# A fused AdaLN block of attention and FFN in fp32: the row maxima go from score rows to subtraction through DRAM, all loads go to SyncE's queue, the prologue joins the written order, and that order is new

## The chip, the cores and the metric

The kernel runs on one core of a Trainium2 chip. The core has five engines with queues of their own: TensorE (PE, matrix products and transposes by a product with the identity), VectorE (DVE), ScalarE (ACT), GpSimd (POOL) and SyncE (SP), which in this kernel does nothing but start DMAs. ACT can start DMAs too. PE reads its operands from SBUF and writes to PSUM, which has eight banks of 2 KB per partition.

The metric is the time of one execution in device microseconds (us), the median of several.

## The reference, cut to what matters

```python
mod = (_silu(L0_c) @ L0_wmod).reshape(8, 6, 1, 256)
sa, ca, ga, sb, cb, gb = (mod[:, k] for k in range(6))
ga = (2 * (ga >= 0) - 1) * jnp.maximum(jnp.abs(ga), 0.25)   # gb likewise
h = _layernorm(x) * (1 + ca) + sa                      # x: (8, 1024, 256)
scores = jnp.einsum('nsd,ntd->nst', h * w_lhs, h * w_rhs)
x = x + ga * jnp.einsum('nst,ntd->nsd', softmax(scores, axis=2), h)
h = _layernorm(x) * (1 + cb) + sb
x = x + gb * (relu(h @ W1 + b1) @ W2 + b2)             # 256 -> 1024 -> 256
```

Everything is fp32. There are eight batches of 1024 rows. The score matrix of a batch is symmetric, since both sides carry the same `h` and the two weights only multiply its columns.

## The kernel before, in words

**Tiles.** The 1024 rows of a batch are `NT` = 8 tiles of `P` = 128 rows; two halves of `HALF` = 512 rows (`g` = 0, 1) are loaded, stored and given to the FFN as one. `V` = 32 is the side of the blocks that DVE's transpose turns.

**Attention of one batch.** Of the scores, PE computes the upper part of the matrix (L520), ACT copies it out of PSUM (L529), and the lower part is its mirror: DVE transposes the 32 × 32 blocks into `T_m` (L555), SP writes them to DRAM as `D_m` in four DMAs (L393) and reads them back in their new places into `sc` (L399). Batch 0 mirrors by PE (L577) instead. For the product with `h` the index that is summed over must lie in the partitions; by the symmetry, the subtraction therefore works on the columns of the matrix that answer to a row tile, 8 blocks with the other index in the partitions and the 128 rows along the free dimension. So the maximum `m` of a row tile, 128 values in 128 partitions (`row_max`, DVE, L603), has to stand along the free dimension of every partition: `max_turn` (L606) lets PE transpose the broadcast column into a bank, `pm` (L608), and `subtract` (L611, DVE, L615) subtracts it from these 128 × 1024 scores with `pm` read from PSUM. ACT takes the exponential (L624).

Two rows form a pair for the product with `h`: `pair_begin` (`pp`, L692; sums into `W`, L701 and L704), `left_sums` (POOL, L717 and L722, the sums `s` of the two exponentials), `pair_end` (`pr` and `pq`, L746: the products are saved Strassen-fashion by sums of operands), `pair_out` (DVE, L763 to L786: divides by the row sum and adds to `x`).

**FFN.** Its input is normed, transposed through DRAM in 32 × 32 blocks (DVE `T_f`, L405; four writes `D_f`, L393; one read `X_f`, L399), modulated into `hT` (L898 on DVE, L900 on ACT) and into POOL's sums `hs` (L911). The first layer is made of the units `pa`, `pb`, `pe` (L923), whose sums DVE adds up (L944), ACT passes through the relu (L1005) and POOL sums further into `ft` (L1019). The second layer is `ya`, `yb`, `yc` (L923); DVE adds them to `Y` (L1049) and so frees the banks, and POOL adds the result to `x` (L1122); `y_out` (L1125) stores 512 KB. The last batch does its second layer otherwise: it loads gated weights `w2g` and `rows` (`load_last`, L1131) and multiplies directly (`py`, L1161).

**Preparation of the next batch.** While batch b is in its attention, the rows of batch b+1 are loaded (`load_x`, L168; six half-batch buffers), normed (DVE statistics L324, ACT L330 to L363), transposed through DRAM like the FFN's input (`T_a`, `D_a`, `X_a`), and multiplied by gate rows (POOL L849, L853) that `load_rows` (L318) spreads over the partitions, 256 KB, into one of two buffers. `load_x` and `load_rows` are issued on ACT's queue by default.

**Order.** Four tables of tokens, `ZERO`, `FIRST`, `MIDDLE` (five times) and `LAST`, give the order of everything after the prologue. `period` (L1457) goes through a table; each token takes the next part of one piece of work, and `:n` names the PSUM bank. A period holds the attention of batch b, most of the FFN of batch b−1 and the preparation of batch b+1. `pin` (L147) then makes every engine execute its instructions in just this order, so an instruction that waits holds all that stand behind it on its engine. The tokens needed below: `S`, `H` score products; `M` mirror parts; `R` row maximum; `T` the spreading of the maximum; `U` subtraction; `E` exponential; `B`, `C`, `L`, `D`, `O` the pair's steps; `a`, `b`, `e` first-layer units; `y*` second layer, with `yo` the store; `fk` and `fh` the FFN's transposition and `hT`; `lx`, `lr` the loads of `x` and of gate rows; `xp` POOL's first use of these; `lw` the load for the last layer. A `+` marks work of the next batch.

The prologue (L1197 to L1305: loads, modulation, norms and transposes of batch 0, first scores) is straight-line code ahead of the tables, in which `any_bank` hands out PSUM banks in turn and three warming matmuls of zeros (L227) stand around the transposes of `c` (L243).

Of the kernel before, what the change touches and what calls it, by code (L numbers as in the profile page):

```python
# [19 lines left out]
GATE_MIN = 0.25  # L20
ZERO = """
pa1 pa1 pa0 pa1 R2 H3:3 N2:4 M2:0 E1 H5:7 lx0 N2 M2 H4:1 S3:6 H5 p0:7 pa0 pa1 pa0 S3 H4
pr1 H3 M5:4 pa0 T2:5 g:1 M4:0 M3:2 pr0 R3 pn0 pn1 U2 M3 pn0 pn0 pn0 p0 M5 pn1 pn0 E2 g
pn1 T3:3 R4 p1:2 U3 pb0 p0 p1 pn1 T4:5 p2:3 M4 H6:6 pb0 pb0 E3 pn1 U4 E4 H6 pb1 pb1 pb0
p1 pb1 R6 R5 p2 M6:7 p3:4 p3 p1 p2 pb1 T6:3 T5:1 pl0 U5 pl0 p2 H7:2 m:6 px0 M6 U6 H7 px0
E5 R7 p4:0 S1+:2 p4 m p3 p4 pl1 pl1 T7:7 px1 E6 U7 p0 p3 S0+:3 px1 H0+:1 H1+:5 S0+ p5:6
fr0 H1+ S1+ E7 H0+ M1+ M0+ R0+ fn0 p5 p7:5 p6:3 p5 fn0 fn0 fn0 fh0 p4 xp1 xp1 xt0 xt0 ps
xt1 fh0 fh0 p7 p6 p6 p7 fh0 xp0 M1+ M0+ p5 p7 p6 xp0 xp0 xp0 xt0 xt0 xt1 xt1 xt1 fh0 rs
rs rs xp1 M0+ M1+ rs xp1 fh0
"""  # L30
FIRST = """
a00:1 S3:4 H2:3 T0:0 lx1 S2:6 S3 b00:5 fr1 pa0 fn1 H2 fn1 pa0 R1 fn1 H3:3 a00 S2 e02:4
b00 T1:2 a00 fn1 H3 a02:3 a00 R2 pa0 U0 pa0 M3 M2 M2 e00:6 a00 H4:5 fn1 e00 lr e00 U1
a00 E0 a00 H4 pr0 a02 r00 pn0 fk1 e02 fk1 pn0 E1 b02:5 e00 b02 a02 B0:0 e02 pa1 C0 M3 L0
pa1 a00 pn0 pn0 a02 e02 M4 M2 M3 fk1 fk1 M4 H5:5 a02 D0:1 D0:2 a02 R3 l02 pn0 pb0 pb0
r02 pb0 B0 C0 l00 L0 D0 L0 D0 t02 T2:6 H5 ya0:7 L0 t00 t02 a02 a02 t00 U2 E2 ya0 yb0:5
O0 T3:6 D0 R4 t00 O0 ya0 B2:0 ya0 fh1 U3 E3 a10:6 ya0 O0 pa1 M5 t02 yb0 pa1 O0 fh1 fh1
t00 L2 fh1 xp0 D2:5 ya0 ya0 t02 xt0 pr1 pn1 O0 a10 pn1 pn1 M4 M5 pb0 yc0:4 pn1 ya0 pn1
H6:2 C2 B2 yc0 pb1 pb1 L2 T4:1 D2:7 yc0 C2 xp0 fh1 fh1 xt0 L2 xt1 L2 a10 D2 R5 yg0 H6
a10 T5:0 U4 D2 D2 yc0 M6 e10:3 pb1 e12:2 M5 O2 Q0 O2 M6 U5 b10:1 b10 O2 E4 pl0 px0 yg0  # L40
e10 pl0 a10 a10 H7:0 B4:4 yt0 E5 r10 e12 px0 O2 O2 Q0 pb1 M6 yt0 yt0 a12:1 C4 a12 e10
e10 a12 e12 a12 b12:7 l10 B4 H7 yt0 xp0 b12 Q2 Q2 R6 xt0 L4 a12 D4:3 D4:7 xt1 xt0 t10 ps
L4 L4 L4 t10 pl1 yd0 px1 C4 a12 e12 a10 D4 S0+:4 D4 T6:2 fr0 a10 fn0 R7 O4 t10 yd0 t10
U6 r12 l12 t12 a12 D4 O4 T7:2 ya1:5 O4 U7 pl1 px1 E6 H0+:6 fn0 a12 S0+ ya1 E7 S1+:4
yb1:7 t12 H0+ fn0 fn0 xt1 xp0 B6:6 C6 ya1 L6 t12 xt1 xp1 H1+:1 O4 M0+ fn0 t12 S1+ O4 Q4
fk0 yb1 fk0 B6 ya1 yc1:3 ya1 ya1 M0+ fk0 D6:7 R0+ T0+:0 ya1 fk0 fh0 yc1 Q4 M0+ yo0 yg1
H1+ U0+ D6:4 yc1 C6 yc1 lx0 E0+ yg1 ya1 fh0 L6 L6 xp1 D6 D6 O6 fh0 L6 D6 R1+ M1+ O6 O6
fh0 rs rs fh0 M1+ fh0 xp1 xp1 rs rs O6 M1+ yt1 O6 yt1 Q6 Q6 yt1 yt1
"""
MIDDLE = """  # L50
S2:2 H3:6 a00:3 b00:5 H2:0 a00 S2 B0:2 H2 e00:1 T1:0 C0 B0 e00 S3:4 a00 a00 fr1 M2 b00
C0 pa0 pa0 a02:2 U1 a02 lr pa0 fn1 H4:5 e00 pa0 a00 e00 a00 e02:7 a02 R2 E1 pr0 fn1 H4
a00 L0 b02:5 S3 H3 fn1 fn1 fn1 D0:1 a00 M3 L0 yd1 b02 M2 fk1 e02 a02 r00 a02 e02 D0:6
l00 pn0 a02 e02 l02 M2 pn0 yd1 L0 t00 T2:0 D0 t00 t00 a02 D0 L0 U2 R3 fk1 O0 M4 yo1 M3
ya0:3 D0 T3:5 M3 H5:4 fk1 U3 lx1 pn0 a02 r02 t02 ps t02 ya0 O0 pn0 ya0 H5 pn0 yb0:5 ya0
E3 O0 pa1 pb0 fk1 pb0 pb0 M4 M4 pa1 ya0 t02 t02 H6:7 O0 pa1 R4 fh1 M5 O0 yb0 E2 Q0 ya0
xp0 t00 xt0 fh1 fh1 fh1 fh1 fh1 L2 H6 ya0 B2:4 ya0 yc0:0 M6 T4:3 C2 yc0 U4 pa1 pb0 pl0
pr1 M6 D2:5 a10:1 a10 M5 M5 b10:2 D2:6 yc0 pn1 R5 pn1 pn1 B2 yg0 pn1 pn1 E4 px0 pl0 L2
L2 D2 L2 pb1 D2 a10 a10 D2 pb1 b10 C2 yc0 O2 a12:3 O2 O2 O2 B4:0 e10:4 T5:6 a10 pb1 a12
e10 px0 M6 O2 pb1 R6 U5 a10 a12 e10 C4 E5 a10 e10 a12 yg0 Q2 a10 e12:4 a12 Q2 xp0 L4 L4  # L60
xp1 H7:1 L4 L4 xt0 xt1 e12 pl1 a12 e12 D4:2 e12 b12:6 D4:5 T6:7 a12 S0+:4 b12 D4 B4 Q0
yt0 H7 px1 r12 r10 a12 l12 l10 px1 U6 E6 fr0 xt0 R7 D4 yt0 D4 C4 yt0 yt0 pl1 O4 fn0 O4
O4 fn0 fn0 H0+:3 T7:7 S1+:0 fn0 O4 U7 S1+ S0+ fn0 H0+ E7 yb1:6 B6:7 xp0 t12 xt1 t10 xp0
t10 H1+:5 t12 t10 xt0 L6 yd0 yd0 t10 L6 ya1:3 D6:4 C6 ya1 ya1 D6:1 xp1 t12 rs t12 L6 L6
fk0 M0+ fk0 yb1 O4 B6 D6 R0+ C6 ya1 M0+ fk0 yo0 M0+ fk0 ya1 T0+:7 yc1:6 ya1 ya1 D6 yc1
fh0 U0+ H1+ O6 M1+ M1+ fh0 R1+ yc1 yc1 fh0 xt1 xp1 xp1 xt1 rs rs fh0 fh0 fh0 rs D6 yg1
ya1 lx0 yg1 E0+ O6 yt1 O6 Q4 Q4 yt1 O6 O6 Q6 M1+ yt1 Q6 yt1
"""
LAST = """
b00:2 S3:6 H2:0 S2:3 H2 a02:5 T1:0 e00:1 B0:7 a00:4 S2 e00 fr1 C0 e00 M2 R2 U1 S3 a00  # L70
a00 b00 a00 e00 a02 B0 E1 H3:3 a00 fn1 C0 a00 fn1 H3 b02:0 b02 M3 l00 e02:1 H5:6 a00 a02
L0 e02 fn1 H5 fn1 a02 e02 T2:7 a02 H4:3 M2 M2 M3 yd1 M3 fn1 a02 a02 D0:2 a00 fk1 fk1 L0
L0 yd1 yo1 r02 r00 t00 H4 a02 e02 M5 U2 yb0:3 D0:6 D0 fk1 M4 fk1 M4 M5 R3 R4 l02 E2 t00
B2:1 H6:7 T3:5 t00 t02 fh1 L0 t02 H6 ya0:0 D0 O0 fh1 D0 O0 O0 M6 O0 ya0 U3 M4 M6 yb0 O0
C2 ya0 b10:6 ya0 t02 B2 fh1 fh1 E3 t02 ya0 ya0 t00 yc0:7 T4:4 Q0 M5 L2 fh1 L2 yc0 U4 ya0
e10:2 L2 R6 a10:4 L2 fh1 a10 yc0 D2:5 a10 b10 C2 yc0 E4 yg0 R5 ya0 e10 a10 yg0 yt0 yt0
D2:0 D2 e10 e10 D2 a12:7 O2 Q0 D2 O2 O2 a12 l10 O2 a10 a12 a10 r10 e12:0 H7:6 T5:2 e12
H7 O2 U5 a10 a10 Q2 B4:1 Q2 a12 e12 a12 t10 yt0 yt0 E5 C4 b12:5 M6 fr0 B4 fn0 a12 a12
r12 R7 e12 b12 l12 fn0 a12 C4 t10 L4 L4 yd0 D4:2 L4 L4 D4:3 D4 D4 O4 T7:5 fn0 fn0 fn0 D4
T6:1 U6 E6 U7 fk0 O4 fk0 E7 t10 O4 t12 yd0 yb1:7 lw yo0 ya1:6 B6:5 t12 ya1 ya1 ya1 fk0  # L80
fk0 L6 t12 D6:4 L6 C6 D6:0 D6 ya1 O4 t10 L6 D6 O4 fh0 fh0 B6 ya1 yb1 C6 L6 t12 yc1:1 yc1
D6 O6 O6 O6 O6 Q4 yc1 Q4 O6 Q6 ya1 lw fh0 e00+:7 a00+:5 Q6 fh0 lw lw fb fh0 lw a02+:3
b00+:0 fr1+ a00+ b00+ a00+ ya1 e00+ lw a00+ fh0 e00+ fn1+ e00+ b02+:0 yc1 a00+ e02+:1
a02+ a00+ l00+ e02+ r00+ a02+ a00+ fn1+ a02+ fn1+ fn1+ yg1 lw fb e02+ lw e02+ b02+ fb lw
a02+ z3:2 a00+ z0:7 fn1+ fk1+ fk1+ z2:1 a02+ fk1+ fk1+ z1:4 a02+ r02+ l02+ z2 a02+ z0
fh1+ z3 fh1+ fh1+ e10+:0 a10+:6 e10+ yg1 a10+ yt1 z0 fh1+ fb fh1+ fh1+ z1 b10+:3 fb fb
fb b10+ z3 yt1 yt1 z2 a10+ e10+ a10+ z1 e10+ a12+:2 a10+ e12+:4 a12+ a12+ a10+ a10+
b12+:5 fb b12+ e12+ l10+ a12+ a12+ e12+ a12+ a10+ e12+ z5:5 r10+ z6:6 a12+ r12+ l12+
a12+ z4:7 z6 z4 z5 z4 z6 z5 z3 yt1 yd1+ yd1+ yo1+ z6 z1 z5 z7:3 z7 z7 z7
# [5 lines left out]
def adaln_block_kernel(  # L95
# [43 lines left out]
    turn = deque([4, 5, 6, 3, 7])  # L139

    def any_bank(name):
        turn.rotate(-1)
        return bank(turn[-1], name)

# [23 lines left out]
    def load_x(b, g, queue=nc.scalar):  # L168
        x_t[b, g] = ring(two, [P, TH, D], "x", 6, f"x_{b}_{g}", 2 * b + g)
        queue.dma_start(  # L170
            out=x_t[b, g],
            in_=x[b, ts(g, HALF), :].rearrange("(t p) d -> p t d", p=P),
        )
# [194 lines left out]
    def prepare_norm(b, g, tiles=range(TH)):  # L368
# [85 lines left out]
    def prepare_turn(b, g, vector=True):  # L454
# [26 lines left out]
        return left  # L481

# [1022 lines left out]
```

## Time and profile before

| | us |
|---|---|
| median of 3 runs (756.27 to 761.42) | 759.52 |
| profiled execution, whole | 760.63 |
| profiled execution, span from first to last instruction | 758.8 |
| POOL `s` 128x512 (L717), mean of 28 | 1.27 |
| PE second-layer or first-layer matmul 128x256 (L923), mean | 0.38 |
| DVE maximum of a row tile (L603), mean of 64 | 1.20 |
| ACT exponential of a row tile (L624), mean of 64 | 1.06 |

In the profile, a line such as `L603 DVE TENSOR_REDUCE m<-sc 128x1 f32<-128x1024 f32 x64 | 76.7, 1200 | 1.6 <-ACT sc L529 1.6` says: the instruction of line 603 on DVE read `sc` (128 partitions by 1024 elements) and wrote `m`; 64 of them were busy 76.7 us, 1200 ns each; the engine stood idle for 1.6 us just ahead of them, and what ended this was ACT's writing of `sc`. In a timeline, the columns are start (us), duration (us), engine, line, operation, out<-in and how many instructions run as one group; a group's duration reaches from the start of its first to the modelled end of its last, so neighbouring groups of PE overlap. A DMA line says how many were issued, the size of one, and the median time from issue to landing. The traffic with DRAM is 124 GB/s over the span, and one profiled issue on SP lasts 0.43 us in the median; before, SP issues 496 DMAs and ACT 20.

### The profile page before, as it was taken

Reading aid. Unit: us, or ns where it says so; the run is one execution under the profiler, and the core shown is the slowest. Engines: PE = TensorE matmul, PEld = TensorE weight load, DVE = VectorE, ACT = ScalarE, POOL = GpSimd, SP = SyncE. Lnnn points to the kernel's source line nnn. Section 1 sums busy time; section 2 is a strip of 40 time slices with the busy share of each in tenths; the row PEclk is TensorE's granted clock in tenths of the full one; section 3 lists DMA queues with packets and bytes.
Section 4 is the critical chain, followed back from the end, with each engine's and each line's share of the span. In section 5 each row is a group of like instructions: output and inputs, shape, how many; then the busy total and the mean of one; then the engine's idle time right before and its main releaser. Section 6 shows DMA issues by size and latency. Waiting matters only on the chain.

```text
span 758.8 us, 11945 instructions
## 1 busy us (share of the span) xinstructions
PE 748.0 (99%) x4044; PEld 626.8 (83%) x4044; DVE 527.7 (70%) x1138; ACT 394.5 (52%) x741; POOL 506.7 (67%) x509
## 2 busy tenths in 40 slices
PE   8999999999999999999999999999999999998998
PEld 4687789788888888887898888978888888987887
DVE  7886877858785786848877587767868586674431
ACT  4562746536465465635657254663656446361541
POOL 3723695957849685696838968399684967577231
PEclk9999999999999999999999999999999999999999
DMA  8134333256525554255632655335552645114122
GB/s 307 43 111 117 105 112 98 65 152 187 155 67 153 172 162 115 71 169 165 184 96 78 181 160 160 99 104 177 166 142 65 183 119 147 30 52 153 28 80 88
DMA packets 106213, 95.22 MB, mean 125 GB/s; under 512 B 29700, under 2 KB 98848, under 8 KB 106152
## 3 DMA queue, kind: packets, MB, share of 16 engines
q1 hardware_dynamic: 98408, 85.81, 39.7%
q10 hardware_dynamic: 7744, 8.65, 3.6%
q8 instruction: 32, 0.52, 0.3%
q14 instruction: 29, 0.24, 0.1%
HBM read 50.62 MB, written 43.81 MB: 124 GB/s over the span
## 4 chain that ended last, share of the span: by engine, by line
PE 89%; DVE 5%; DMA 3%; SPq 1%; ACT 1%; issue 1%; POOL 0%; DVEq 0%; ACTq 0%; POOLq 0%
PE psc L520 16%; PE pa L923 13%; PE ya L923 11%; PE pr L746 9%; PE pe L923 7%; PE pq L746 6%; PE yc L923 6%; PE pp L692 6%; PE po L641 4%; PE py L1161 4%; PE pb L923 3%; PE yb L923 3%; DVE f L944 1%; PE pm L608 1%; DVE pT L615 1%
## 5 line engine op out<-in xcount | busy, mean ns | idle before, releaser
L520 PE MATMUL psc<-rT,lT 128*128 128x512 f32 (+3 forms) x384 | 137.1, 486 | 0.0
L717 POOL TENSOR_TENSOR s<-pT 128x512 f32<-128x512 f32 x28 | 35.6, 1270 | 109.8 <-ACT pT L624 107.7
L520 PEld LDWEIGHTS psc<-rT,lT 128*128 128x128 f32 x384 | 67.0, 191 | 36.0 <-issue 24.4
L615 DVE TENSOR_TENSOR pT<-sc,pm 128x1024 f32<-128x1024 f32 x64 | 77.3, 1208 | 18.9 <-PE pm L608 9.4
L603 DVE TENSOR_REDUCE m<-sc 128x1 f32<-128x1024 f32 x64 | 76.7, 1200 | 1.6 <-ACT sc L529 1.6
L624 ACT ACTIVATE pT<-pT 128x1024 f32<-128x1024 f32 x64 | 67.1, 1056 | 14.8 <-DVE pT L615 12.0
L1005 ACT ACTIVATE f<-f 128x512 f32<-128x512 f32 (+1 forms) x64 | 52.2, 844 | 31.4 <-DVE f L944 31.4
L923 PE MATMUL pa<-hT,w 128*128 128x256 f32 x256 | 66.1, 381 | 0.8 <-DVE f L944 0.4
L911 POOL TENSOR_TENSOR hs<-hT 128x256 f32<-128x256 f32 x32 | 23.1, 731 | 63.3 <-DVE hT L898 58.0
L923 PE MATMUL pa<-hs,w1s 128*128 128x256 f32 x256 | 64.8, 379 | 0.0
L529 ACT COPY sc<-psc 128x512 f32<-128x512 f32 (+3 forms) x96 | 44.2, 479 | 38.1 <-PE psc L520 36.5
L692 PEld LDWEIGHTS pp<-xg,pT 128*128 128x128 f32 x448 | 56.9, 192 | 6.2 <-issue 2.4
L692 PE MATMUL pp<-xg,pT 128*128 128x129 f32 x448 | 59.1, 275 | 0.7 <-DVE Y L1049 0.7
L746 PEld LDWEIGHTS pq<-tsum,pT 128*128 128x128 f32 x448 | 57.4, 192 | 2.3 <-issue 0.2
L746 PE MATMUL pq<-tsum,pT 128*128 128x128 f32 (+1 forms) x448 | 59.1, 275 | 0.0
L939 ACT COPY k<-pa 128x512 f32<-128x512 f32 x64 | 36.8, 581 | 40.5 <-PE pa L923 33.9
L923 PE MATMUL yc<-f,w2s 128*128 128x256 f32 x224 | 54.1, 385 | 3.5 <-DVE Y L1049 3.5
L849 POOL TENSOR_TENSOR x<-x,rows 128x256 f32<-128x256 f32 x64 | 46.3, 734 | 11.7 <-ACT rows L1274 10.0
L1019 POOL TENSOR_TENSOR ft<-f 128x512 f32<-128x512 f32 x28 | 35.7, 1275 | 27.6 <-ACT f L1005 27.6
L923 PEld LDWEIGHTS pa<-hT,w 128*128 128x128 f32 x256 | 46.0, 190 | 9.6 <-issue 2.4
L923 PE MATMUL ya<-ft,w 128*128 128x256 f32 x224 | 53.6, 383 | 0.0
L923 PEld LDWEIGHTS pa<-hs,w1s 128*128 128x128 f32 x256 | 46.7, 190 | 6.6 <-ACT k L939 0.2
(161 smaller groups left out, 1761.3 us busy)
## 6 DMA issues: line engine op xcount, KB each, us to landing
D_f<-T_f SPq DMA_DIRECT2D x60, 128.0 KB, 2.4
X_f<-D_f SPq DMA_DIRECT2D x15, 512.0 KB, 3.4
D_a<-T_a SPq DMA_DIRECT2D x56, 128.0 KB, 2.4
D_y<-T_y SPq DMA_DIRECT2D x56, 128.0 KB, 2.6
Y<-D_y SPq DMA_DIRECT2D x14, 512.0 KB, 3.4
out_dram<-x SPq DMA_DIRECT2D x14, 512.0 KB, 4.3
X_a<-D_a SPq DMA_DIRECT2D x13, 512.0 KB, 3.7
x<-in_L_attn_x_dram ACTq DMA_DIRECT2D x12, 512.0 KB, 3.7
```

What stands on the lines that cost most here:

```text
L520: nc.tensor.matmul(psc[:, : hi - lo], lhsT=lT_t[b, i // TH][:, k, ts(i % TH, P)], rhs=rT_t[b, n][:, k, lo - n * HALF : HALF], start=(k == ...
L529: nc.scalar.copy(score_row(b, i)[:, lo // V : hi // V, :], box["p"][:, : hi - lo].rearrange("p (n v) -> p n v", v=V),)
L603: nc.vector.tensor_reduce(m, score_row(b, i), AX.XY, ALU.max)
L615: nc.vector.tensor_tensor(pT.rearrange("p j (a v) -> p j a v", v=V), score_columns(b, i), pm[:, :P].rearrange("p (j a v) -> p j a v", j=1, ...
L624: nc.scalar.activation(pT_t[b, i], pT_t[b, i], AF.Exp)
L692: nc.tensor.matmul(box["pp"][:, h * XS : (h + 1) * XS], lhsT=pT_t[b, i][:, h * TH + t, :], rhs=xg_t[b][:, h * TH + t, P : P + XS], start=( ...
L746: nc.tensor.matmul(out, lhsT=lhs[:, t, :], rhs=rhs[:, t, :], start=(t == 0), stop=(t == TH - 1),)
L849: nc.gpsimd.tensor_tensor(xr, xr, rows_t[b][:, 1, :], ALU.add)
L923: nc.tensor.matmul(out, lhsT=lhsT, rhs=rhs, start=first, stop=True, skip_group_check=True)
L939: nc.scalar.copy(k, src)
L1005: nc.scalar.activation(part, part, AF.Relu)
L1019: nc.gpsimd.tensor_tensor(out, x, y, op)
```

## The change

- **The maximum's way.** For batches 1 to 7 `max_turn` is gone. `row_max` writes the maxima of the two rows of a pair into the two columns of one 128 × 2 tile. `max_rows` writes this tile to DRAM (8 bytes from each partition) and reads the 256 values back into every partition, 128 KB, as `mr`; both DMAs are SP's. `subtract` reads its row out of `mr` (every second element) in SBUF. The token `T` exists for even rows only and has two parts, write and read. Batch 0 keeps the transposes.
- **The loads.** `load_x` and `load_rows` are issued by SP; the gate rows have one buffer instead of two.
- **The prologue** is cut into parts with tokens of their own and stands in the table `ZERO`; `any_bank` and the straight-line code go. In it, the transposes of `c` (`0c`) come ahead of the three warming matmuls (`0w`).
- **The tables** are all new. Middle table before: `lr` is token 26, `yo1` 86, `lx1` 95. After: `yo1` 54, `lx1` 82, `lr` 163. In the last table the store `yo0` moves from the place just ahead of `lw` and of the FFN's writes to the end of the table.

The arithmetic is unchanged, and so is the number of all other instructions of DVE and POOL.

```diff
-    def load_x(b, g, queue=nc.scalar):
+    def load_x(b, g, queue=nc.sync):
...
     def rows_tile(b):
-        rows_t[b] = ring(two, [P, 2, D], "rows", 2, f"rows_{b}", b)
+        rows_t[b] = ring(two, [P, 2, D], "rows", 1, f"rows_{b}", b)
         return rows_t[b]

-    def load_rows(b, queue=nc.scalar):
+    def load_rows(b, queue=nc.sync):
...
     def row_max(b, i):
-        m = ring(work, [P, 1], "m", 3, f"m_{b}_{i}")
+        if (b, i // 2) not in max_t:
+            max_t[b, i // 2] = [ring(work, [P, 2], "m", 3, f"m_{b}_{i}", (b * NT + i) // 2)]
+        m = max_t[b, i // 2][0][:, i % 2 : i % 2 + 1]
         nc.vector.tensor_reduce(m, score_row(b, i), AX.XY, ALU.max)
-        max_t[b, i] = m
-
-    def max_turn(b, i, q=2):
+
+    def max_turn(b, i, q):
+        m = max_t[b, i // 2][0][:, i % 2 : i % 2 + 1]
         pm = bank(q, f"pm_{b}_{i}")
-        nc.tensor.transpose(pm[:, :P], max_t.pop((b, i)).to_broadcast([P, P]), ident)
-        pT_t[b, i] = pm
+        nc.tensor.transpose(pm[:, :P], m.to_broadcast([P, P]), ident)
+        pT_t[b, i] = pm[:, :P]
+
+    def max_rows(b, i):
+
+        at, box = (b * NT + i) // 2, {}
+
+        def write():
+            box["D"] = ring(dram, [P, 2], "M", 4, f"M_{b}_{i}", at)
+            nc.sync.dma_start(out=box["D"], in_=max_t[b, i // 2][0])
+
+        def back():
+            R = ring(work, [P, P, 2], "mr", 2, f"mr_{b}_{i}", at)
+            nc.sync.dma_start(
+                out=R.rearrange("p s r -> p (s r)"),
+                in_=box["D"].rearrange("s r -> (s r)").partition_broadcast(P),
+            )
+            for r in range(2):
+                pT_t[b, i + r] = R[:, :, r]
+
+        return [write, back]
...
     def subtract(b, i):
...
             score_columns(b, i),
-            pm[:, :P].rearrange("p (j a v) -> p j a v", j=1, v=V).to_broadcast([P, NT, NV, V]),
+            pm.rearrange("p (j a v) -> p j a v", j=1, v=V).to_broadcast([P, NT, NV, V]),
             ALU.subtract,
...
         for i in range(0 if b == 1 else 1, NT):
-            w[f"T{i}"] = [lambda q, i=i: max_turn(b, i, q)]
+            if i % 2 == 0:
+                w[f"T{i}"] = max_rows(b, i)
             w[f"U{i}"] = [lambda i=i: subtract(b, i)]
...
-            w["T0+"] = [lambda q: max_turn(n, 0, q)]
+            w["T0+"] = max_rows(n, 0)
```

The stretch of the middle table from the first maximum of the second pair to its products, before and after:

```diff
-R2 E1 pr0 fn1 H4
-a00 L0 b02:5 S3 H3 fn1 fn1 fn1 D0:1 a00 M3 L0 yd1 b02 M2 fk1 e02 a02 r00 a02 e02 D0:6
-l00 pn0 a02 e02 l02 M2 pn0 yd1 L0 t00 T2:0 D0 t00 t00 a02 D0 L0 U2 R3 fk1 O0 M4 yo1 M3
-ya0:3 D0 T3:5 M3 H5:4 fk1 U3 lx1 pn0 a02 r02 t02 ps t02 ya0 O0 pn0 ya0 H5 pn0 yb0:5 ya0
-E3 O0 pa1 pb0 fk1 pb0 pb0 M4 M4 pa1 ya0 t02 t02 H6:7 O0 pa1 R4 fh1 M5 O0 yb0 E2 Q0 ya0
-xp0 t00 xt0 fh1 fh1 fh1 fh1 fh1 L2 H6 ya0 B2:4
+R2 pn0 M4 D0:6 ya0:5 C0 t00 t02 L0 H6:0 a02 lx1 L0 t02 t00
+B0 ya0 pn0 D0 D0 ya0 pa1 pa1 t00 D0 M3 fk1 pa1 M4 a02 pa1 t02 R3 pr1 pn0 pn1 pn0 t02 T2
+R4 pn0 pn1 H6 fk1 T2 C0 pb0 M6 ya0 O0 M5 O0 O0 O0 pb0 R5 yb0:0 U3 ya0 fh1 yc0:6 ya0 yc0
+U2 E3 O0 a10:1 ya0 H7:7 yg0 fh1 E2 pn1 ya0 yc0 M5 M6 fh1 yb0 yc0 L2 pn1 B2:5
```

## The prediction, made before the changed kernel had run

> **What bounds the kernel now.** I read the page's busy shares first, then its chain by engine, then the table of windows, then the few places where TensorE (PE) stands still.
>
> ```profile
> span 758.8 us, 11945 instructions
> PE 748.0 (99%) x4044; PEld 626.8 (83%) x4044; DVE 527.7 (70%) x1138; ACT 394.5 (52%) x741; POOL 506.7 (67%) x509
> PEclk9999999999999999999999999999999999999999
> PE 89%; DVE 5%; DMA 3%; SPq 1%; ACT 1%; issue 1%; POOL 0%; DVEq 0%; ACTq 0%; POOLq 0%
> ```
>
> PE is busy 748.0 of 758.8 us at its full clock and carries 89% of the chain that ends last. By windows of 90 us from 170 to 620, PE is busy 89.6 to 90.0, POOL 66 to 70, DVE 65 to 67, ACT about 50: there, only fewer matmuls or a new stall can change the time. The 10.8 us in which PE does nothing lie at the ends: 76.07 busy of the 80 us from 620 to 700, 55.47 of the last 58.8.
>
> The profiled execution took 760.63 us, 1.8 more than its span and 1.1 more than the median of the runs, 759.52. I sum against 760.6 and take 1.1 off at the end.
>
> **Transposes removed (gain).** The order of the two programs shows 64 transposes `pm` before and 8 after (batch 0 keeps its own); all other matmuls stay. A transpose lasts 0.27 us, but the one here costs less:
>
> ```profile
> 274.24 1.05 PE L746 MATMUL pq<-tsum,pT 128*128 128x128 f32 x8
> 275.13 0.27 PE L608 MATMUL pm<-ident,m 128*128 128x128 f32 x1
> 275.24 1.06 PE L746 MATMUL pr<-tsum,pT 128*128 128x128 f32 x8
> ```
>
> The next group starts 0.11 us after the transpose, inside its recorded 0.27. 56 × 0.11 = **−6.2**. (56 × 0.274 = 15.3 is the far end; the overlap speaks against it.) The waits of PE for `m` go as well: 0.3 us in all.
>
> **The gap in the last table (gain).** Before, the last attention period has this:
>
> ```profile
> 692.77 0.81 PE L923 MATMUL yc<-f,w2s 128*128 128x256 f32 x3
> 693.42 1.05 PE L746 MATMUL pr<-xg,pT 128*128 128x128 f32 x8
> 697.99 3.05 PE L923 MATMUL yc<-f,w2s 128*128 128x256 f32 x8 [3.52 <-DVE Y L1049]
> 700.84 2.56 PE L923 MATMUL ya<-ft,w 128*128 128x256 f32 x8
> ```
>
> ```profile
> 696.18 0.55 DVE L898 TENSOR_SCALAR hT<-X_f,modT 128x512 f32<-128x512 f32 x1 [10.32 <-DMA X_f<-D_f]
> 696.64 0.42 DVE L1049 TENSOR_TENSOR Y<-yb,Y 128x256 f32<-128x256 f32 x1
> ```
>
> DVE waits 10.32 us at `hT` for a block read; the adds `Y` that free PE's banks stand behind it. PE idles 3.52 us, and the two groups after it take 3.05 and 2.56 in place of 1.89 each, 1.8 more. The read is late because SyncE (SP) had just queued the 1 MB of `w2g`, 256 KB of `rows` and a 512 KB store ahead of the writes `D_f`. In the new table that store (`yo0`) stands at the very end and the other one (`yo1`) behind the read; the loads stay ahead. From write to `hT` took 12.6 us; the PE work now standing between them is five groups `pq` and `pr` of 0.89 and four second-layer groups of 1.73, 11.4 us, and without 0.5 MB to share the queue the trip should be shorter than that. −3.5 − 1.8 = **−5.3**, bounds 0 and −5.3.
>
> The second such trip (row block 1 of batch 7) took 8.7 us before, from issue at 717.5 to `hT` at 726.2, and had 12 us of last-layer matmuls over it; the new order leaves 9.5 (three groups `pa` of 0.86 and four `py` halves of 1.73), and the write is later in the row: **+1.5**, from 0 to 5.
>
> **Prologue.** The transposes of `c`, which started at 3.46 us behind the first of three warming matmuls, now stand ahead of all three. So the remaining 4.9 us of cold warming matmuls run after `c` arrives, and the first modulation product, at 6.28, starts up to 1.9 later; since both first transposed blocks now come before the first score row, part of it is won back: **+1.0**. From +1.9 down to −2, because what the new order of the norms saves no row shows.
>
> **The new way of the maxima.** For 56 rows in 28 pairs it adds a write of 128 × 8 bytes and a broadcast read of 128 KB, both on SP. No row shows 8-byte pieces. The rows nearest to it:
>
> ```profile
> D_m<-T_m SPq DMA_DIRECT2D x28, 32.0 KB, 1.7
> sc<-D_m SPq DMA_DIRECT2D x7, 128.0 KB, 2.6
> D_m<-T_m SPq DMA_DIRECT2D x28, 16.0 KB, 2.9
> X_f<-D_f SPq DMA_DIRECT2D x15, 512.0 KB, 3.4
> rows<-rows_d ACTq DMA_DIRECT2D x6, 256.0 KB, 4.5
> ```
>
> The write takes 1.7 to 2.9 (I take 2.9, the smallest piece), the read 2.6 to 4.5 (2.6, same size), one issue 0.43: 5.9 in all, against some 1.5 from max to subtraction before (the longest wait for `pm` on DVE). DVE executes in written order, so what matters is what stands between the max of the pair's second row (`R3`) and its first subtraction (`U3`). In the middle table this is one `rs` 0.49, two maxima 2.4, a pair sum 0.28, two `T_a` 1.38, two `T_m` 0.75 and four pair outputs 1.41: 6.7 us. So the trip is covered on DVE. Tighter is PE: from `R3` to the pair's products `B2` lie 9.9 us of matmuls, and the way through is 0.43 + 2.9, an issue of the 512 KB read `X_f` that stands between write and read (0.34), 0.43 + 2.6, `U3`, a `Y` add and `U2` (2.84), `E2` 1.06 = 10.6. That is 0.7 late per period if DVE stands level with PE; it has 25 of 90 us free and mostly stands ahead, so I take **+1.0** over seven periods, with bounds 0 and (read behind all 3.4 us of `X_f`) 4.1 × 7 = 29. Nothing below 0: the old wait is counted already.
>
> A rule of the Trainium skill speaks against the small write: "DMA: Bandwidth & Descriptors", section Specifications, asks at least 512 B a piece, below which the engine reads, changes and writes back. The rows above show no such rise from 32 KB to 16 KB beyond 1.2 us, and nothing at 8 bytes. If by this rule the write doubled to 5.8, the tight pair would be 2.9 later in each period and the sum some 20 higher.
>
> **Loads and queues.** ACT loses 18 issues of 0.59 (12 of `x`, 6 of `rows`), 10.6 us of an engine 52% busy: 0. SP gains 56 + 18 issues × 0.43 = 32 us on 496 × 0.43 = 213, so 32% of the span: 0 by itself; its only price is order, and that is the `X_f` above. The loads of `x` now wait on SP for the 4.3 us store of their buffer, with the M writes queued behind; the middle table puts store and load 28 tokens apart, so 0, and up to 0.5 a period without. `rows` has one buffer and its load waits for POOL's last use in the batch before; it goes just ahead of the next use. POOL is free 20 of 90 us, and a load of 4.5 fits: 0.
>
> **Subtraction from SBUF.** `U` now has two SBUF inputs instead of one and a PSUM one. Own speed: `xg` (two SBUF inputs, 128x1024) took 1.215 us with POOL idle, `U` 1.208: 0. Beside POOL see the second rival.
>
> **Sum.** 760.6 − 6.2 − 5.3 + 1.5 + 1.0 + 1.0 = 752.6; less 1.1 = **751.5**.
>
> **Rivals.**
>
> *The trip shows.* If DVE does not stand ahead at the tight pair, 0.7 to 2 late per period, say 1.3 × 7 = 9: 751.5 + 9 − the 1.0 counted = **759.5**, no change. For: DVE's stats of new `x` tiles wait for a load behind a store just before `R3`. Against: those 25 free us.
>
> *The port* (the other side). In the trace, DVE instructions of one size differ by where their inputs lie:
>
> ```profile
> L786 DVE SCALAR_TENSOR_TENSOR x<-W,rl,x 128x128 f32<-128x128 f32 x28 | 18.5, 661 | 0.0
> L786 DVE SCALAR_TENSOR_TENSOR x<-pr,rl,x 128x128 f32<-128x128 f32 x28 | 9.8, 351 | 1.0
> ```
>
> With `W` and `x` both in SBUF it takes 661 ns (341 to 1421), with `pr` in PSUM always about 350: it waits for POOL, 0.31 on average. 56 × 0.31 = 17 more on DVE. That alone hides (545 of 759). On the path it counts where results of POOL reach PE with no room: the starts of `ya` and of `pr` follow POOL's `ft` and `s` within 0.2 us at about three places a period. If two of these come late by one `U` (1.21, POOL waiting in its turn) and two `U` stand on the path themselves (0.31), it is 3.0 × 7 = 21: 751.5 + 21 = **772**; with only the DVE part, 0.62 × 7 = 4.3: 756. It decides from about 2.2 us a period on (15 over seven). Against: POOL has 20 of 90 us free, so a late step is caught up unless it falls at those places.
>
> The Trainium skill, "SBUF — State Buffer", section Who interferes with whom, goes further than the row: a VectorE instruction with two SBUF inputs and a GpSimd instruction that reads SBUF shut each other out for a whole instruction, so POOL would wait as well as DVE, which no row here shows for POOL. By it POOL's 506.7 would grow by up to 56 × 1.21 = 68, and the sum would be the rival's upper one.
>
> *Everything hides and the small costs are gains:* no +1.0 for the trip, no +1.5, the prologue at its lower end of −2: 752.6 − 5.5 − 1.1 = **746**. For: DVE's and POOL's free time. Against: the two ends have no such room.
>
> *It doesn't do what it says* is excluded: the order shows 56 transposes gone and 18 loads moved.
>
> **How the numbers follow.** Forecast 50%, its own range 747 to 758; the trip shows 22%; the port 16%; everything hides 12%. The predicted time is the forecast's. Within 1% of 759.5 is 751.9 to 767.1 (about what a measurement can tell from no change). Faster: all of the last case and 28 points of the forecast, 40%. Same: 22 points of the forecast and 18 of the trip, 40%. Slower: the port and 4 points of the trip, 20%. A range of 744 to 770 leaves out some of the port and of the tails of the others.
>
> **What would show it.** Right: PE busy near 740 in a span near 751; the group before a removed transpose followed by the next after 0.89; no idle PE of 3.5 us in the last period; DVE's `U` about 1.21 with little idle time for `mr`. Wrong: `U` near 1.5 and POOL's 128x512 sums well above 1.27 us (the port); DVE idle before `U` with the read `mr` as releaser, and PE waiting in `pp` for `pT` (the trip); a first score row later than 14.5 us (prologue; it began at 12.63).

## The result, and the profile after

The changed kernel takes 813.2 us in the median of four runs (812.1 to 815.8) against 759.2 before: 1.072 times the time before (95% interval 1.067 to 1.077), 54 us slower. The prediction was 751.5, at most 770.

The page of the changed kernel, in the parts shown of the kernel before: span, busy engines, TensorE's granted clock in tenths, and the chain that ended last by engine and by line.

```profile
span 810.5 us, 11849 instructions
PE 760.9 (94%) x3988; PEld 627.2 (77%) x3988; DVE 542.0 (67%) x1138; ACT 394.9 (49%) x741; POOL 541.8 (67%) x509
PEclk9999998999999999999999999999999999899999
PE 43%; DMA 20%; DVE 14%; POOL 11%; ACT 4%; issue 4%; SPq 2%; DVEq 0%; POOLq 0%; ACTq 0%
PE pa L948 9%; PE psc L544 7%; DMA mr<-M 6%; DMA M<-m 5%; PE pe L948 4%; POOL ft L1044 4%; PE po L666 3%; PE py L1186 3%; DVE pT L640 3%; PE pr L771 3%; DMA D_m<-T_m 3%; PE pp L717 3%; PE ya L948 3%; DMA X_f<-D_f 2%; PE pb L948 2%
```

PE carried 89% of the chain before, now 43%. DMA has 20%, the maxima's read and write alone 11%, and POOL, which had 0%, 11%. PE is idle for 50 us (before 11), and though 56 transposes are gone its busy time grew by 13, in part because its matmuls ran at a lower clock after some of the stops (mean granted clock 0.983, before 0.998).

Who waits, in the table of waits of the changed kernel (us in all, times, the longest):

```profile
ACT pT L649 <- DVE pT L640: 86.8, 34, 6.3
POOL hs L936 <- DVE hT L923: 72.9, 15, 10.7
POOL s L742 <- ACT pT L649: 60.3, 14, 14.3
DVE pT L640 <- DMA mr<-M: 57.5, 18, 7.7
PE pa L948 <- DVE hT L923: 8.9, 5, 2.5
PE pa L948 <- ACT sc L553: 8.4, 4, 2.4
```

And the same waits in the kernel before:

```profile
POOL s L717 <- ACT pT L624: 107.7, 21, 12.7
POOL hs L911 <- DVE hT L898: 58.0, 15, 23.5
ACT pT L624 <- DVE pT L615: 12.0, 11, 1.7
DVE pT L615 <- PE pm L608: 9.4, 8, 1.5
```

`DVE pT <- DMA mr<-M` is the source: DVE stands at 18 of the 56 subtractions for the broadcast read, 57.5 us in all, where it stood 9.4 us for the transposed maximum. ACT's exponentials stand behind the subtraction, 86.8 us in place of 12.0. POOL's long waits are no sign of the loss: before, `hs` and `s` waited 58.0 and 107.7 us, with PE busy 99% of the time. The two PE lines are the largest groups of its stops.

One such place, the first subtraction of batch 3 (token `U0+`), in the timeline of the changed kernel, first SP (the two DMAs of the pair), then DVE, ACT and PE (start, duration, what; in brackets the idle time before it and what ended it):

```profile
268.93 0.34 SPq L623 DMA_DIRECT2D M<-m  x1
...
273.08 0.33 SPq L627 DMA_DIRECT2D mr<-M  x1
...
277.86 2.08 DVE L640 TENSOR_TENSOR pT<-sc,mr 128x1024 f32<-128x1024 f32 x1 [3.94 <-DMA mr<-M]
...
279.98 1.06 ACT L649 ACTIVATE pT<-pT 128x1024 f32<-128x1024 f32 x1 [6.29 <-DVE pT L640]
...
281.89 0.60 ACT L553 COPY sc<-psc 128x512 f32<-128x512 f32 x1
...
282.54 1.77 PE L948 MATMUL pa<-hT,w 128*128 128x256 f32 x4 [2.42 <-ACT sc L553]
```

The maximum is ready at 268.9, the write is issued at once, SP can issue the read only when the write has landed, 4.15 us later, and 4.78 us after that the subtraction starts: 8.9 us where the forecast had 5.9. DVE idles 3.94 of it, ACT 6.29. Behind the exponential in ACT's order stand two copies `k` of first-layer sums and the copy of the next scores out of PSUM (281.89); PE waits 2.42 us until this copy has freed a bank. The other place of the middle table is `U3`, in the same timeline:

```profile
313.11 1.23 DVE L640 TENSOR_TENSOR pT<-sc,mr 128x1024 f32<-128x1024 f32 x1 [2.71 <-DMA mr<-M]
314.26 0.54 DVE L923 TENSOR_SCALAR hT<-X_f,modT 128x512 f32<-128x512 f32 x1
...
314.85 1.13 PE L948 MATMUL pa<-hT,w 128*128 128x256 f32 x4 [2.52 <-DVE hT L923]
```

Here the FFN's `hT` stands behind the waiting subtraction, and PE waits 2.52 us for `hT`, not for the pair.

What the DMAs take (count, size of one, median us from issue to landing), and the groups whose durations changed (busy us, mean ns, idle before):

```profile
X_f<-D_f SPq DMA_DIRECT2D x15, 512.0 KB, 5.6
mr<-M SPq DMA_DIRECT2D x28, 128.0 KB, 4.6
rows<-rows_d SPq DMA_DIRECT2D x7, 256.0 KB, 5.0
M<-m SPq DMA_DIRECT2D x28, 1.0 KB, 3.9
```

```profile
L640 DVE TENSOR_TENSOR pT<-sc,mr 128x1024 f32<-128x1024 f32 x56 | 80.3, 1435 | 63.8 <-DMA mr<-M 57.5
L742 POOL TENSOR_TENSOR s<-pT 128x512 f32<-128x512 f32 x28 | 40.6, 1449 | 60.4 <-ACT pT L649 60.3
```

The subtraction takes 1.44 us in place of 1.21, POOL's sum `s` 1.45 in place of 1.27, and POOL is busy 35 us more in all. `X_f` lands after 5.6 us, before after 3.4.

### The profile page after: what moved, and what is told of

Read it like the earlier page. It is cut to its first block, busy times and chain, and to the rows that moved or that the text cites. A ratio compares the mean times of both kernels' runs of the same rounds, so it can differ in the third digit from the quotient of the medians.

```text
span 810.5 us, 11849 instructions
## 1 busy us (share of the span) xinstructions
PE 760.9 (94%) x3988; PEld 627.2 (77%) x3988; DVE 542.0 (67%) x1138; ACT 394.9 (49%) x741; POOL 541.8 (67%) x509
## 4 chain that ended last, share of the span: by engine, by line
PE 43%; DMA 20%; DVE 14%; POOL 11%; ACT 4%; issue 4%; SPq 2%; DVEq 0%; POOLq 0%; ACTq 0%
PE pa L948 9%; PE psc L544 7%; DMA mr<-M 6%; DMA M<-m 5%; PE pe L948 4%; POOL ft L1044 4%; PE po L666 3%; PE py L1186 3%; DVE pT L640 3%; PE pr L771 3%; DMA D_m<-T_m 3%; PE pp L717 3%; PE ya L948 3%; DMA X_f<-D_f 2%; PE pb L948 2%
## 5 line engine op out<-in xcount | busy, mean ns | idle before, releaser
L544 PE MATMUL psc<-rT,lT 128*128 128x512 f32 (+3 forms) x384 | 139.7, 498 | 2.2 <-ACT sc L553 2.2
L640 DVE TENSOR_TENSOR pT<-sc,mr 128x1024 f32<-128x1024 f32 x56 | 80.3, 1435 | 63.8 <-DMA mr<-M 57.5
L649 ACT ACTIVATE pT<-pT 128x1024 f32<-128x1024 f32 x64 | 67.4, 1055 | 87.7 <-DVE pT L640 86.8
L544 PEld LDWEIGHTS psc<-rT,lT 128*128 128x128 f32 x384 | 70.3, 195 | 42.0 <-issue 25.7
L948 PE MATMUL pa<-hT,w 128*128 128x256 f32 x256 | 69.4, 396 | 21.0 <-DVE hT L923 8.9
L874 POOL TENSOR_TENSOR x<-x,rows 128x256 f32<-128x256 f32 x64 | 54.5, 862 | 51.0 <-issue 20.2
L936 POOL TENSOR_TENSOR hs<-hT 128x256 f32<-128x256 f32 x32 | 23.1, 727 | 92.6 <-DVE hT L923 72.9
L742 POOL TENSOR_TENSOR s<-pT 128x512 f32<-128x512 f32 x28 | 40.6, 1449 | 60.4 <-ACT pT L649 60.3
L948 PEld LDWEIGHTS pa<-hT,w 128*128 128x128 f32 x256 | 47.9, 196 | 37.4 <-ACT sc L553 12.0
L948 PE MATMUL pa<-hs,w1s 128*128 128x256 f32 x256 | 68.2, 391 | 1.5 <-POOL hs L936 1.1
L1030 ACT ACTIVATE f<-f 128x1024 f32<-128x1024 f32 (+1 forms) x64 | 52.3, 841 | 23.6 <-DVE f L969 23.6
L1147 POOL TENSOR_TENSOR x<-x,Y 128x512 f32<-128x512 f32 x28 | 39.3, 1416 | 18.3 <-DMA Y<-D_y 18.2
```

Of the source, the lines that this page charges most:

```text
L544: nc.tensor.matmul(psc[:, : hi - lo], lhsT=lT_t[b, i // TH][:, k, ts(i % TH, P)], rhs=rT_t[b, n][:, k, lo - n * HALF : HALF], start=(k == ...
L640: nc.vector.tensor_tensor(pT.rearrange("p j (a v) -> p j a v", v=V), score_columns(b, i), pm.rearrange("p (j a v) -> p j a v", j=1, v=V).t ...
L649: nc.scalar.activation(pT_t[b, i], pT_t[b, i], AF.Exp)
L742: add(box["s"], *halves(pT_t[b, i + 1]), ALU.add)
L874: nc.gpsimd.tensor_tensor(xr, xr, rows_t[b][:, 1, :], ALU.add)
L948: nc.tensor.matmul(out, lhsT=lhsT, rhs=rhs, start=first, stop=True, skip_group_check=True)
```

## The experiments

Fifteen kernels ran, each beside the kernel before on the same chip, whose median was 758.7 to 759.3 each time. Only e_pe, e_trip, e_loads, e_yo0 and e_swap do the whole computation; the others subtract the constant 30 in place of the row maximum in batches 1 to 7. The theory: DVE's wait for the trip is most of the loss, the port a part. The rivals: the port is most of it; the new order and the loads on SP are. In each, "the ratio" is to the kernel before, with its 95% interval.

**Neither trip nor port (e_pe).** In the changed kernel,

```diff
-            if i % 2 == 0:
-                w[f"T{i}"] = max_rows(b, i)
+            w[f"X{i}"] = [lambda q, i=i: max_turn(b, i, q)]   # token X{i}:bank ahead of U{i}
```

> The changed kernel, its order, its loads and its prologue, but the row maxima of batches 1 to 7 spread by TensorE transposes again, each some four tokens ahead of its subtraction, in a bank that is free there; the DMA write and the broadcast read are gone. So neither the trip nor a second SBUF input is left. If the trip (write 3.9 + read 4.6 us instead of the 5.9 in all of the forecast, DVE idle 57.5 us for it) and the port (POOL busy 35 us more, subtractions 1.44 us instead of 1.21) make up the loss, it takes about 760: 813 less 54, perhaps some us less for the better end. If the new order and the loads on SyncE's queue make up the loss, it stays above 795.

776.6 us, ratio 1.024 (1.020 to 1.028). So 37 of the 54 us go with the new way of the maxima, but 17 stay, where 0 were expected. What holds it is in its PE waits:

```profile
PE pq L774 <- DVE pT L643: 8.5, 5, 1.7
```

That is a bank: `pq` waits until a subtraction has read the maximum out of the bank that `pq` needs next. The new tables gave out the banks without one for the maxima, so this kernel isn't the new order by itself; e_single and e_act answer that.

**The port alone (e_port).**

```diff
-        pm = pT_t.pop((b, i))
+        pm = fixed[:, :, i % 2] if b > 0 else pT_t.pop((b, i))   # fixed: SBUF, 30.0
```

> The changed kernel without write and read: each subtraction of batches 1 to 7 takes a constant (30) from an SBUF tile in place of the row maximum, so two SBUF inputs stay and nothing waits for a DMA. The maxima are still computed, and no TensorE transposes come back. Left against e_pe: only the port (and 56 transposes, some 6 us, less). Trip theory: the port alone costs 2 us a period in late POOL sums, so about 760 + 14 - 6 = 768. Port theory: most of the loss stays, 790 or more.

762.0, ratio 1.004 (1.002 to 1.006): below 768, and far from 790. The port isn't most of the loss. It is there, though; the chain of this kernel by engine, and its subtraction:

```profile
PE 70%; POOL 16%; DVE 8%; ACT 3%; issue 2%; DMA 1%; SPq 0%; DVEq 0%; ACTq 0%; POOLq 0%
```

```profile
L642 DVE TENSOR_TENSOR pT<-sc,fixed 128x1024 f32<-128x1024 f32 x56 | 89.0, 1589 | 6.5 <-PE pr L773 6.5
```

POOL is on the chain and a subtraction takes 1.59 us, though nothing waits for a DMA. Which of POOL's sums grow differs: `s` takes 1.28 us here, hardly more than before, `ft<-f` 1.49 in place of 1.28.

**The trip alone (e_trip).**

```diff
+        if b > 0:
+            nc.vector.tensor_copy(tick, mr_t[b, i // 2][:, 0, i % 2 : i % 2 + 1])
         # then as e_pe: subtraction of the transposed maximum in PSUM
```

> As e_pe (maxima by TensorE, one SBUF input), but write and read of the maxima stay as in the changed kernel, and a one-element copy on DVE just ahead of each subtraction reads the tile that came back, so DVE waits for the trip. Left: the trip without the port. Trip theory: most of the loss, 795 to 805 (the 6 us of transposes among it). Port theory: 775 or less.

810.8, ratio 1.068 (1.063 to 1.073): with one SBUF input only, nearly as slow as the changed kernel. The bank waits of e_pe are in it too, so the trip's share is the difference to e_pe, 34 us; some of it comes by the banks that a late subtraction keeps, since PE's waits for subtractions rise from 11.5 to 24.7 us. In e_pe and e_trip, where the subtraction reads PSUM, it takes 1.21 us in the mean, as before, and POOL is busy 508.0 and 507.7 us (before 506.7); in the changed kernel it is 541.8.

**The DMAs without anyone waiting (e_traffic).** As e_port, with write and read left in.

> As e_port (a constant in an SBUF tile), but write and read of the maxima stay on SyncE, and nobody reads what comes back (its tile has one buffer). Left against e_port: the 56 DMAs in SyncE's queue, in which the write waits for the maxima and the read for the write, with other loads and writes behind. If only DVE's own wait for the read counts, the time is that of e_port, within 1%. If it is the queue that makes the FFN's block read and the loads late, it stays 15 us or more above e_port.

776.1, ratio 1.024 (1.020 to 1.028): 14.1 above e_port, and 37.1 below the changed kernel. So DVE's wait is worth 37.1, and the two DMAs cost 14.1 even when nobody waits for them. That is just under the 15 looked for if the queue counts; that the DMAs cost so much by themselves was no part of my theory.

**One SBUF input, no trip (e_single).**

```diff
+            nc.vector.tensor_scalar(pT_view, score_columns(b, i), 30.0, None, ALU.subtract)
```

> As e_port (new order, no write and read, no transposes after batch 0), but the subtraction of the constant is a tensor_scalar with the number in the instruction, so it has one SBUF input only. If the port made e_port lose about 3 us a period (its middle periods last 90.7 us for 87.7 of matmuls, with POOL's sums late), this one takes some 745, if subtractions last about 1.2 us. If the 3 us are something else in the new order, it takes 762 like e_port.

747.6, ratio 0.984 (0.981 to 0.986). So the new order with its prologue and loads is no loss at all, and the port costs 762.0 − 747.6 = 14.4. The size has a doubt both ways: this instruction is shorter than the one it replaces, and it doesn't free POOL wholly (busy 524.0, against 506.7 before and 545.5 in e_port).

```profile
L641 DVE TENSOR_SCALAR pT<-sc 128x1024 f32<-128x1024 f32 x56 | 53.9, 962 | 10.3 <-PE pr L777 10.1
```

**The same two in the old order (e_old_port, e_old_single).** In the kernel before, the tokens `T` of batches 1 to 7 dropped, the subtraction as in e_port or as in e_single.

> The kernel before, in its own order, without the 56 transposes: the subtractions of batches 1 to 7 take the constant 30 from a small SBUF tile in place of the row maximum (the maxima are computed and not used). Two SBUF inputs, no wait for a maximum. If the port costs as much in the old order as in the new, 3 us a period, it takes 759 - 6 + 21 = 774; if the old order has more room for POOL, 759 or less.

> As e_old_port, but the constant stands in a tensor_scalar with one SBUF input. Left against the kernel before: only the 56 transposes and the waits for them are gone. By the forecast's 0.11 us each it takes 759.5 - 6.2 = 753; if a transpose costs its recorded 0.27 us, 744.

768.4, ratio 1.012 (1.008 to 1.015), and 751.4, ratio 0.989 (0.986 to 0.992). The 56 transposes and the waits for them were worth up to 7.9 us, and the port costs 17.1 in the old order. Not all of the 7.9 need be theirs: the subtraction is shorter here as well, and the stop at `yc` in the last table fell from 3.5 to 1.7 us. From batch 1's third score row to batch 7's the two traces differ by 5.1 us for some 48 transposes, 0.11 each.

**Loads back on ACT (e_loads).**

```diff
-    def load_x(b, g, queue=nc.sync):
+    def load_x(b, g, queue=nc.scalar):
```

and `load_rows` likewise.

> The changed kernel with load_x and load_rows on ACT's queue again (18 DMAs), all else as changed. If the loads ahead of them in SyncE's queue are what makes the maxima's trip long, it takes 800 or less; if the trip is long by its own two landings, 808 to 815, as changed.

835.0, ratio 1.099 (1.093 to 1.104): slower by another 22 us, against both expectations. The loads on SP don't make the trip long: its two DMAs land after 3.9 and 4.6 us here too. Among PE's waits there are 7.1 us at `yb` for ACT's score copies, which the changed kernel hasn't; where the rest of the 22 comes from isn't shown.

**One token in the old last table (e_yo0).**

```diff
-T6:1 U6 E6 U7 fk0 O4 fk0 E7 t10 O4 t12 yd0 yb1:7 lw yo0 ya1:6
+T6:1 U6 E6 U7 fk0 O4 fk0 E7 t10 O4 t12 yd0 yb1:7 lw ya1:6
...
-z7:3 z7 z7 z7
+yo0 z7:3 z7 z7 z7
```

> The kernel before with one token moved: in the last table the 512 KB store yo0 leaves its place between the weight load and the FFN's block writes and goes to the table's end, as in the changed kernel. By the forecast's second term it gains between 0 and 5.3: TensorE's stop of 3.5 us before yc goes and the two groups behind it take 1.9 us each; I expect 754 to 756. If the read is late for the 1.25 MB of loads alone, nothing changes.

756.2 (12 runs), ratio 0.9965 (0.995 to 0.998): 2.7 us faster, and the only kernel with the whole computation here that beats both. In its timeline of PE the stop of 3.52 is 0.63, and the group takes 1.99 in place of 3.05:

```profile
694.97 1.99 PE L923 MATMUL yc<-f,w2s 128*128 128x256 f32 x8 [0.63 <-DVE Y L1049]
```

**Banks or transposes (e_act).**

```diff
-        nc.tensor.transpose(pm[:, :P], m.to_broadcast([P, P]), ident)
+        nc.scalar.copy(pm[:, :P], fixed)                # batches 1 to 7
```

> As e_pe, but the tile in PSUM that the subtraction reads is filled with a constant by a short copy on ACT instead of a TensorE transpose of the maxima, in the same banks at the same places. e_pe took 776.6, some 21 more than e_single (747.6) and the price of the transposes (7.9 by e_old_single) make. If the transposes themselves hold TensorE up (they wait for a maximum), this one takes some 750. If it is the banks, which were given out anew by the changed order and leave no room for the extra tile, it takes about 768.

Ratio 1.016 (1.010 to 1.022), some 771 (767.0 to 776.0 in the runs compared): far from 750, so it is the banks, though ACT's 56 copies are extra work. PE waits as in e_pe, in this kernel's table of waits:

```profile
PE pq L779 <- DVE pT L648: 9.1, 5, 1.8
```

**What stands behind the wait (e_swap).** In the changed kernel's middle table:

```diff
-R5 yb0:0 U3 ya0 fh1 yc0:6 ya0 yc0 U2 E3
+R5 yb0:0 ya0 fh1 yc0:6 ya0 yc0 U3 U2 E3
```

> The changed kernel with one token moved in the middle table: U3 goes behind the FFN's modulation hT and the Y add, just ahead of U2. In the changed kernel DVE stands at U3 for the read, and hT, whose data has landed, stands behind it, so that TensorE waits 1.3 to 2.5 us for hT in each of the five middle periods. If the trip's cost is what stands behind the waiting subtraction in DVE's order, this gains 7 to 12 of the 813. If the time is set by the pair itself (its exponentials and products come late), it gains nothing.

802.4, ratio 1.056 (1.053 to 1.060): 10.8 less than 813.2. Not all of it is the edit's: in the two traces the five periods with the edited table are 7.6 us shorter together, but batch 1's period, whose table is the same in both, is 6.9 shorter too (98.4 in place of 105.2). `hT` no longer waits for the maxima, and in its timeline PE's `pa` follows without a stop:

```profile
300.08 1.89 PE L948 MATMUL yc<-f,w2s 128*128 128x256 f32 x8
301.81 1.07 PE L948 MATMUL pa<-hT,w 128*128 128x256 f32 x4
```

**Why unused DMAs cost 14 us (e_free, e_write, e_read, e_plain).** All from e_traffic:

```diff
-            nc.sync.dma_start(out=box["D"], in_=max_t[b, i // 2][0])
+            nc.sync.dma_start(out=box["D"], in_=fixed[:, 0])       # not in e_read, e_plain
...
-                in_=box["D"].rearrange("s r -> (s r)").partition_broadcast(P),
+                in_=still.rearrange("s r -> (s r)").partition_broadcast(P),   # not in e_write
+                in_=still,                                          # e_plain: [P, 256] in DRAM
```

> As e_traffic (56 DMAs whose result nobody reads), but the write takes its 1 KB from a constant tile and the read takes a tile written once at the start, so neither waits for anything: the same transfers at the same places in SyncE's queue, without a hold of the queue. e_traffic lost 14 us against e_port (762.0). If that is SyncE standing at the write (for the maxima) and at the read (for the write's landing) with the mirror's writes and reads behind, this one takes 762 to 765. If it is the transfers themselves, 774 to 778.

> As e_free, without the 28 reads: only the 28 writes of 8 bytes from each of 128 partitions are left, and they wait for nothing. e_free takes 772.6, e_port (neither) 762.0. If the small pieces of the write hold up the other transfers, 770 or more; if the broadcast reads do, 762 to 764.

> As e_free, without the 28 writes: only the 28 broadcast reads of 128 KB, in which every partition takes the same 1 KB, are left. If the reads hold up the other transfers, 770 or more, and X_f lands after 5 us or more in place of 3.6; if the writes do, 762 to 764.

> As e_read, but each partition reads a 1 KB of its own from a DRAM tile of 128 KB written once at the start, so only the broadcast is gone. If it is the repeated source that makes the read slow (4.6 us here and 5.0 for the 256 KB of gate rows, against 2.4 for a plain 128 KB write and 3.5 for a plain 512 KB read), it lands in 3 us or less and the time falls to 762 to 764; if it is just 128 KB more in the queue, both stay as in e_read.

| | us | ratio (95%) | above e_port |
|---|---|---|---|
| e_free: both, nothing waits | 772.6 | 1.018 (1.015 to 1.021) | 10.6 |
| e_write: the 8-byte write alone | 766.3 | 1.009 (1.007 to 1.011) | 4.3 |
| e_read: the broadcast read alone | 766.5 | 1.010 (1.007 to 1.012) | 4.5 |
| e_plain: the same 128 KB, plain | 762.4 | 1.004 (1.003 to 1.006) | 0.4 |

Neither the write nor the read does it alone, which is what each of the two expectations looked for; they cost about the same, and together about their sum. SP's holds are the difference of e_traffic and e_free, 3.5 of the 14.1; their intervals overlap, so it may be less. Landings in e_port (none of the two), then in e_write, then in e_read, then in e_plain:

```profile
X_f<-D_f SPq DMA_DIRECT2D x15, 512.0 KB, 3.6
X_a<-D_a SPq DMA_DIRECT2D x13, 512.0 KB, 4.1
```

```profile
X_f<-D_f SPq DMA_DIRECT2D x15, 512.0 KB, 5.7
M<-fixed SPq DMA_DIRECT2D x28, 1.0 KB, 4.9
```

```profile
X_a<-D_a SPq DMA_DIRECT2D x13, 512.0 KB, 5.3
mr<-still SPq DMA_DIRECT2D x28, 128.0 KB, 3.7
```

```profile
X_a<-D_a SPq DMA_DIRECT2D x13, 512.0 KB, 4.3
mr<-still SPq DMA_DIRECT2D x28, 128.0 KB, 3.4
```

With the write of 1 KB in 128 pieces the 512 KB read `X_f` lands after 5.7 us in place of 3.6, and after 5.5 and 5.6 in e_traffic and e_free, which have the write too. With the broadcast read alone `X_a` lands after 5.3 in place of 4.1, with the plain one after 4.3. But in e_free, with write and broadcast read, it is 4.2; and `X_f` lands after 4.0 in e_read, not after the 5 that I had expected there, and after 4.3 in e_plain. So the prices are measured, that of the broadcast against the plain read too; that they come about by the late neighbours is likely for the write and not shown for the read.

## Why the prediction was wrong, by its steps

The loss in parts, each the difference of two medians:

| step | from, to | us |
|---|---|---|
| 56 transposes and their waits removed | before, e_old_single | −7.9 |
| new order, prologue, loads on SP | e_old_single, e_single | −3.7 |
| second SBUF input (port) | e_single, e_port | +14.4 |
| write and read in the queue, unused | e_port, e_traffic | +14.1 |
| DVE's wait for the read | e_traffic, changed | +37.1 |

The parts are what each costs in this sequence. They are not independent: from e_pe to e_trip the wait and the DMAs together cost 34, not 51, in a kernel that PE's banks already hold up.

**Transposes, −6.2: right.** 7.9 with the waits and what else e_old_single changes; the interval is 6 to 10, and the recorded 0.27 a piece (15.3) is out. The 0.11 a piece stands in the trace of e_old_single.

**The gap in the last table, −5.3: right in kind, too large.** e_yo0 gained 2.7 (1.5 to 3.8). The stop and the slow groups went as read from the trace.

**Second trip +1.5: not separated; prologue +1.0: nothing came of it.** With the gap they were to give −2.8; order, prologue and loads gave −3.7. The first score row began at 14.74 us, 2.1 later than before and past the 14.5 named as a sign of being wrong:

```profile
7.13 1.88 PE L288 MATMUL pmr<-wm,scT 128*8 128x512 f32 x4
13.56 1.34 PE L484 MATMUL pth<-ident,xg 128*128 128x128 f32 x8
14.74 6.61 PE L544 MATMUL psc<-rT,lT 128*128 128x512 f32 x16
```

Of the 2.1, 0.85 is the later first modulation product (7.13, before 6.28), and 1.2 the second group of transposes, which now comes ahead of that row. By batch 1's third score row both are won back: it begins at 73.2 in the changed kernel, 72.8 in e_single, 72.9 before.

**The new way of the maxima, +1.0 with bounds 0 and 29: the step that failed.** It cost 37.1 in waits and 14.1 in the queue (813.2 − 776.1 and 776.1 − 762.0). Three things were wrong in it.

- The length. "Write 2.9, read 2.6" took the rows nearest in size. In the changed kernel they land after 3.9 and 4.6 us (the issue of the read follows that of the write by 4.2 in the median of the 28 pairs). The read's nearest row was of its kind, not its size: `rows`, the other broadcast, 4.5, which stood in the same fence and was kept for the bound only.
- The cover. "The trip is covered on DVE" compared 5.9 with the 6.7 us of DVE work between `R3` and `U3`. With 8.9 the same comparison fails: at the `U3` shown above the subtraction starts 9.1 us after the end of `R3`, 6.4 of them DVE's work and 2.71 idle. And "it has 25 of 90 us free and mostly stands ahead, so I take +1.0" turned the argument round: an engine that stands ahead of PE reaches its wait early and idles there; being ahead gives room to PE only if nothing that PE needs soon stands behind the wait.
- The consumer. I followed the pair to its own products `B2`. In the five middle periods PE stopped at `hT` and at a score bank, which have nothing to do with the maxima and stand behind the subtraction in DVE's and ACT's written order. `pp` waiting for `pT`, the sign that the forecast had named, came once, 3.2 us in batch 1's period; PE's other two long stops there, 3.5 and 3.7, were at a first-layer sum and a pair output, both behind a waiting subtraction. e_swap shows it for `hT`: with one subtraction moved past two short DVE instructions the stop is gone, and the five periods that this touches are 7.6 us shorter. I had listed `X_f` as queued on SP, but not what is queued on DVE behind `U3`.

The bound of 29 was too low as well, since it took one tight place a period and no cost for the transfers themselves. "Loads and queues: 0 by itself" counted SP's issues and asked nothing of what the new DMAs do to the landing of others.

By the Trainium skill, "DMA: Bandwidth & Descriptors", section Specifications, pieces under 512 bytes are read, changed and written back. The write landed after 3.9 us, not after 5.8 as I had worked out for a doubling, but e_write shows a price of 4.3 us of the kernel's time. The runs don't show whether a write-back is the reason.

**The trip as a rival, 759.5: the mechanism, at a quarter of its price.** It was to be 1.3 us in each of seven periods, 9 in all, and the wait alone cost 37.1. Between e_traffic and the changed kernel, from the start of batch 1's third score row to that of batch 2's, 13.0 us were lost; in the five periods after it 3.6 each in the mean (0.7 to 5.5); from there to the end 5.2. These are single executions, and they vary: the first of these periods took 105.2 us in the changed kernel and 98.4 in e_swap, with the same table.

**The port as a rival, 772: right in sign and near in size.** It was priced at 21 and cost 14 to 17. Alone it would have left the time unchanged (e_port, 1.004): it gives back what transposes and order bring. The Trainium skill's rule ("SBUF — State Buffer", section Who interferes with whom) held where the row of before was silent: POOL lost time too, 35 us of the 68 worked out as its limit.

**The chances.** 78 points of 100, the port's 16 among them, stood on cases in which the trip is hidden or nearly so, and 4 on its making the kernel slower. Nothing in the profile carried such a split but the order of instructions that I took for cover.

## What to carry to other kernels

Where a wait is put into an engine with a fixed order, list everything behind it on that engine, and the first thing that the bounding engine needs from that list; the new chain's own end is rarely the tight one. Price a new DMA by the row of its own kind (broadcast, small pieces, plain), then by what it does to the landing of its neighbours in the queue. An engine that runs ahead doesn't hide a wait: it reaches it sooner.

## What the runs showed of the hardware, unexpected

After a stop of 2.4 us PE's clock was lower in one place and not in another. Windows of the changed kernel around the stop at 280 us, then after that at 312 (span; us in it, busy time of PE, PEld, DVE, ACT, POOL; then the granted clock):

```profile
280.00:282.50 2.50, 0.12 (x1) 0.00 (x0) 2.37 (x8) 2.48 (x4) 1.25 (x2) 1.00 0.34 77
282.50:284.50 2.00, 1.96 (x5) 1.59 (x6) 1.13 (x3) 1.74 (x5) 0.00 (x0) 0.60 0.43 172
284.50:286.50 2.00, 2.00 (x7) 1.57 (x6) 1.93 (x6) 1.05 (x2) 0.00 (x0) 0.55 0.50 108
286.50:289.00 2.50, 2.50 (x14) 2.08 (x13) 1.44 (x4) 2.07 (x4) 0.85 (x1) 1.00 0.41 96
...
314.80:317.00 2.20, 2.15 (x10) 1.92 (x11) 2.17 (x4) 2.11 (x4) 2.12 (x2) 1.00 0.05 11
```

After 2.42 us of idle time the clock was 0.60 and 0.55 for some four microseconds, and groups of four matmuls took 1.77 and 1.91 us in place of 1.03; after 2.52 us at 312 it stayed at 1.00. Of the 15 stops of over 1 us in this trace six, of 2.15 to 4.64 us, were followed by a clock of 0.50 to 0.67 over the next two microseconds; after the other nine, one of 3.22 us among them, it was 1.00. So a short stop costs its length or nearly twice it (here 2.42, and 1.8 in the three groups after it), and between 2.15 and 3.22 us its length doesn't tell which.
